# Top-p sets of an attention matrix: sorted lists of segment maxima in place of a 28-step bisection

## The chip, the cores and the metric

One core of a Trainium2 chip runs the whole program. The metric is the device time of one execution in microseconds (us), as a median of several executions. The engines are named PE (TensorE, matrix products), DVE (VectorE), ACT (ScalarE), POOL (GpSimd) and SP (SyncE, which issues most transfers). In the traces here, where all products are float32, each leaves two records (the 8 logits products of a tile are 16 records at 574.39 us of the kernel before), so a count behind PE is twice the number of products in the code.

## The reference, cut to what matters

Four layers work on 4096 nodes with 256 features and a 4096x4096 adjacency matrix, in float32. Layer 1 is the one that the change touches. It makes two attention steps, and each row keeps the smallest set of largest probabilities that reaches 0.9:

```python
def _top_p_attention(X, W1, W2, W3):
    q = X @ W1.T @ W2.T
    k = X @ W3.T
    probs = softmax(q @ k.T, axis=-1)                  # 4096 x 4096
    idx = argsort(-probs, axis=-1)
    sp = take_along_axis(probs, idx, axis=-1)
    cs = cumsum(sp, axis=-1)
    keep_sorted = cs - sp < 0.9                        # sum of all larger ones is below 0.9
    mask = zeros(...).at[rows, idx].set(keep_sorted)
    A = probs * mask
    return A / maximum(A.sum(-1, keepdims=True), 1e-12)

Xf, Xa = X, X
for n in range(2):
    A = _top_p_attention(Xa, W1, W2, W3)
    Xf = R @ Xf                                        # R: row-normalised adjacency + identity
    Xa = A @ Xa
    Z = Z + Xf @ U1[n].T + Xa @ U2[n].T
```

Layer 0 before it and layers 2 and 3 after it are the same in both kernels. Among equal probabilities those with the lower index are kept first. In step 2 this matters: a count on the host, which no run shows, finds some 860 rows with equal values at the border of the set, because rows whose attention keeps a single neighbour become copies of one another.

## The kernel before

A row is one of 128 partitions, and a tile is 128 rows, so each step has 32 tiles. `e` holds a tile's exponentials, 4096 a partition, and there are two such tiles. The threshold is found bit by bit: for each of 28 bits one pass over all 4096 elements sums what lies at or above a candidate. (Cuts are marked.)

```python
T_BASE, T_BITS = 0x30000000, 28

def bisect(e, tgt, cand, bits):
    for b in bits:
        junk = tmp_tile([P, N], BF16)
        f = small.tile([P, 1], F32, name="f")
        nc.vector.scalar_tensor_tensor(junk, e, cand.bitcast(F32), e, op0=OP.is_ge, op1=OP.mult, accum_out=f)
        up = small.tile([P, 1], I32, name="up")
        nc.vector.tensor_scalar(up, f, tgt, float(1 << b), op0=OP.is_ge, op1=OP.mult)
        nc.vector.scalar_tensor_tensor(cand, cand, (3 << b) >> 1, up, op0=OP.bitwise_xor, op1=OP.bitwise_xor)

# ... keep_top: one more pass, then per 1024 columns an equality, a scan, two masks and a sum

def weighted_sum(ps, e, rhs):
    for g in range(NT // 4):
        pt = psum.tile([P, 4, P], F32, name="pt", tag="tp", bufs=2)
        for k in range(4):
            j = g * 4 + k
            nc.tensor.transpose(pt[:, k, :], e[:, j * P:(j + 1) * P], ident)
        eT = work.tile([P, 4, P], F32, name="eT")
        nc.scalar.copy(eT, pt)
        for k in range(4):
            j = g * 4 + k
            nc.tensor.matmul(ps[:, :D], eT[:, k, :], rhs[j], start=(j == 0), stop=(j == NT - 1))

# in attn_step, for each tile I:
            bisect(e, tgt, cand, bits[:8])
            if pending is not None:
                step_out(*pending)                     # output products of the tile before
            adj_matmul(psr, Xf, I)                     # R @ Xf
            if I + 1 < NT:
                nxt = attn_prep(n, I + 1)              # logits and exponentials of the next tile
            bisect(e, tgt, cand, bits[8:])
            rk = keep_top(e, tgt, floor, cand)
            weighted_sum(psa, e, Xa)                   # A @ Xa
```

## Time and profile before

The time is 13,453 us. Cut at the first use of the bisection and at the end of each stage, the span divides like this:

| stretch | us | PE busy | DVE busy | granted PE clock |
|---|---|---|---|---|
| step 1 | 5760 | 29% | 96% | 0.63 |
| step 2 | 5765 | 27% | 96% | 0.62 |
| layer 2 | 830 | 77% | 88% | 0.88 |
| layer 3 | 539 | 99% | 12% | 1.00 |

Layer 0 takes the first 550 us or so. Read the table row by row: the busiest engine of a stretch is the candidate for its bound, and here DVE has no time left in either step. The lines that carry this are shown in the prediction below. One line belongs beside them, the clock granted to TensorE in 40 equal slices of the span, in tenths of full speed:

```profile
PEclk9998555555555555555666666666666666658899
```

TensorE was granted 0.63 and 0.62 of full speed through the two steps. It waits for VectorE there: in step 2 it stood idle for 3984 of 5765 us until VectorE's last masking of a tile was done.

### The profile page before, as it was taken

The page shows a single profiled execution, that of the slowest core. Times are in us where ns is not written, and L with a number is a line of the kernel's source. Part 1 is how long each engine was busy: PE and PEld are TensorE (multiplying, and loading weights), DVE is VectorE, ACT ScalarE, POOL GpSimd, SP SyncE. Part 2 cuts the span into 40 slices and gives each one's busy share as a digit, 9 for nine tenths or more (in the row PEclk, how much of TensorE's full clock was granted, in tenths as well). Part 3 has the DMA queues.
Part 4 walks back from the last instruction along what each step waited for, and adds up shares of the span by engine and source line. Part 5 has one row for each costly group of instructions (what it writes and reads, how often), then busy time and mean ns, then how long its engine had stood idle before and what let it go on. Part 6 is the DMA issues. An engine that isn't in the chain of part 4 may idle for free.

```text
span 13444.6 us, 59326 instructions
## 1 busy us (share of the span) xinstructions
PE 4912.1 (37%) x20320; PEld 3788.8 (28%) x20320; DVE 11941.8 (89%) x11136; ACT 1236.6 (9%) x1897; POOL 1009.2 (8%) x760
## 2 busy tenths in 40 slices
PE   9987221122222221112222222222222222217799
PEld 7766111111111111111222111222211122216678
DVE  1399999999999999999999999999999999998841
ACT  0000000000000000000000000000000000003310
POOL 0000000000000000000111001111100111114420
PEclk9998555555555555555666666666666666658899
DMA  4432000000000000000000000000000000004444
GB/s 141 126 97 77 1 1 1 1 1 1 1 1 1 1 1 1 1 1 4 14 14 14 7 13 14 14 14 14 14 7 13 14 14 14 13 27 157 163 133 132
DMA packets 607406, 430.09 MB, mean 32 GB/s; under 512 B 24832, under 2 KB 573712, under 8 KB 607104
## 3 DMA queue, kind: packets, MB, share of 16 engines
q1 hardware_dynamic: 601600, 419.53, 10.1%
q10 hardware_dynamic: 4608, 4.20, 0.1%
q8 instruction: 161, 2.64, 0.1%
q0 software_dynamic: 896, 2.57, 0.1%
q14 instruction: 141, 1.16, 0.0%
HBM read 415.71 MB, written 10.49 MB: 32 GB/s over the span
## 4 chain that ended last, share of the span: by engine, by line
DVE 77%; PE 14%; issue 4%; POOL 3%; DMA 1%; ACT 0%; SPq 0%; DVEq 0%; ACTq 0%; POOLq 0%
DVE tmp L208 52%; PE acc L105 6%; DVE tmp L229 4%; DVE up L210 3%; PE acc L121 3%; DVE tmp L232 2%; DVE e L233 2%; DVE e L234 2%; DVE tmp L219 2%; PE lg L192 2%; DVE cand L211 2%; DVE tmp L228 1%; POOL rs L142 1%; DVE tmp L342 1%; DVE nm L195 1%
## 5 line engine op out<-in xcount | busy, mean ns | idle before, releaser
L208 DVE SCALAR_TENSOR_TENSOR tmp<-e,cand 128x4096 bf16<-128x4096 f32 x1792 | 8052.4, 4494 | 57.4
L116 PE MATMUL pt<-ident,e 128*128 128x128 f32 x3072 | 534.8, 332 | 8213.8 <-DVE e L234 7817.6
L116 PEld LDWEIGHTS pt<-ident,e 128*128 128x128 f32 x3072 | 451.9, 172 | 8322.7 <-DVE e L234 7866.2
L118 ACT COPY eT<-pt 128x512 f32<-128x512 f32 x768 | 427.5, 588 | 10140.8 <-PE pt L116 10140.6
L121 PE MATMUL acc<-x,eT 128*128 128x256 f32 x4096 | 1112.4, 432 | 55.4 <-ACT eT L118 55.3
L105 PE MATMUL acc<-x,panel 128*128 128x256 f32 x4096 | 933.0, 387 | 57.4 <-DVE y L257 57.4
L121 PEld LDWEIGHTS acc<-x,eT 128*128 128x128 f32 x4096 | 872.0, 219 | 256.0 <-ACT eT L118 118.4
L105 PEld LDWEIGHTS acc<-x,panel 128*128 128x128 f32 x4096 | 787.6, 194 | 179.4 <-DVE y L257 68.7
L275 POOL MEMSET cand<- 128x1 int32 x64 | 6.2, 100 | 9161.5 <-DVE e L233 9161.5
L121 PE MATMUL acc<-xa,eT 128*128 128x256 f32 x2048 | 585.6, 449 | 19.1 <-ACT eT L118 19.1
L192 PE MATMUL lg<-kT,qi 64*128 64x512 f32 x1024 | 527.5, 626 | 3.2 <-ACT e L193 3.2
L121 PEld LDWEIGHTS acc<-xa,eT 128*128 128x128 f32 x2048 | 456.8, 229 | 127.7 <-ACT eT L118 50.3
L105 PE MATMUL acc<-xf,panel 128*128 128x256 f32 x2048 | 488.7, 403 | 4.4 <-DVE y L257 4.4
L105 PE MATMUL acc<-xw,panel 128*128 128x257 f32 x2048 | 477.3, 386 | 12.4 <-DVE xw L74 10.7
L229 DVE TENSOR_TENSOR_SCAN tmp<-ones,last,tmp 128x1024 f32<-128x1024 f32 x192 | 450.9, 2348 | 0.0
L105 PEld LDWEIGHTS acc<-xf,panel 128*128 128x128 f32 x2048 | 418.8, 206 | 68.9 <-DVE y L257 4.8
L210 DVE TENSOR_SCALAR up<-f,tgt 128x1 int32<-128x1 f32 x1792 | 380.7, 212 | 51.0
L105 PEld LDWEIGHTS acc<-xw,panel 128*128 128x128 f32 x2048 | 379.9, 191 | 76.6 <-issue 27.7
L173 DVE TENSOR_SCALAR r<-acc 128x1 f32<-128x1 f32 x32 | 5.1, 159 | 437.5 <-PE acc L105 437.5
L387 DVE TENSOR_TENSOR y<-y,pz 128x256 f32<-128x256 f32 x32 | 13.5, 421 | 420.1 <-PE pz L386 420.1
L341 POOL TENSOR_TENSOR e<-tmp,score_b 128x1024 f32<-128x1024 f32 x128 | 330.4, 2589 | 430.7 <-PE pt L116 211.8
L211 DVE SCALAR_TENSOR_TENSOR cand<-cand,up 128x1 int32<-128x1 int32 x1792 | 285.1, 159 | 54.6
(107 smaller groups left out, 5558.4 us busy)
## 6 DMA issues: line engine op xcount, KB each, us to landing
panel<-in_adjT SPq DMA_DIRECT2D x1024, 256.0 KB, 2.7
tmp<-in_adj SPq DMA_DIRECT2D x128, 512.0 KB, 3.6
tmp<-in_adjT SPq DMA_DIRECT2D x128, 512.0 KB, 4.8
z<-z SPq DMA_DIRECT2D x64, 128.0 KB, 1.9
x<-in_x ACTq DMA_DIRECT2D x32, 128.0 KB, 4.0
out<-o SPq DMA_DIRECT2D x32, 128.0 KB, 1.8
q<-q SPq DMA_DIRECT2D x64, 32.0 KB, 1.8
qi<-q SPq DMA_DIRECT2D x64, 32.0 KB, 2.0
```

The costliest lines, as they stand in the source:

```text
L105: nc.tensor.matmul(ps[:, :n], a[:, k, :], rhs[j], start=(j == 0), stop=(j == NT - 1))
L116: nc.tensor.transpose(pt[:, k, :], e[:, j * P:(j + 1) * P], ident)
L118: nc.scalar.copy(eT, pt)
L121: nc.tensor.matmul(ps[:, :D], eT[:, k, :], rhs[j], start=(j == 0), stop=(j == NT - 1))
L192: nc.tensor.matmul(ps, qi[r, :], kT[r, c * LC:(c + 1) * LC], start=True, stop=True)
L208: nc.vector.scalar_tensor_tensor(junk, e, cand.bitcast(F32), e, op0=OP.is_ge, op1=OP.mult, accum_out=f)
L210: nc.vector.tensor_scalar(up, f, tgt, float(1 << b), op0=OP.is_ge, op1=OP.mult)
L211: nc.vector.scalar_tensor_tensor(cand, cand, (3 << b) >> 1, up, op0=OP.bitwise_xor, op1=OP.bitwise_xor)
L219: nc.vector.scalar_tensor_tensor(junk, e, t, e, op0=OP.is_gt, op1=OP.mult, accum_out=g)
L229: nc.vector.tensor_tensor_scan(cs, ones.to_broadcast([P, CC]), eq, last, op0=OP.mult, op1=OP.add)
L232: nc.vector.scalar_tensor_tensor(eq, cs, tgt, eq, op0=OP.is_lt, op1=OP.mult)
L341: nc.gpsimd.tensor_mul(e[:, cols], a, sb[:, cols])
```

## The change

The intent is to replace 28 passes over 4096 elements by few passes and short lists. Each row is cut into 32 segments of 128. One instruction gives the 8 largest elements of a segment, so 32 of them give 256 candidates. From these, repeated "8 largest" and "replace these 8 by zero" instructions build a sorted list of the largest 40 (step 1) or 64 (step 2). A running sum along the list shows where 0.9 is passed. The largest dropped value `u` then masks the row. In step 2 the sets are wider, so a secant search with three passes first finds a bound `h` above which everything is kept, and the list covers what lies below. The result is only right if no segment hides a ninth element that belongs to the set, if the list was long enough, and if the bound's sum stays below 0.9. These are the proofs. They are counted per tile, and a branch repeats a tile by the old bisection where a row failed. The core of the diff, with cuts marked by "..." and comments added here:

```diff
-    small = ctx.enter_context(tc.tile_pool(name="small", bufs=3))
+    small = ctx.enter_context(tc.tile_pool(name="small", bufs=2))
...
+    def attn_exp(n, I):                    # no row maximum: exp straight from PSUM, with row sums
+        e = epool.tile([P, N], F32, name="e")
+        s8 = small.tile([P, N // LC], F32, name="s8")
+        logits(n, I, lambda c, ps: nc.scalar.activation(e[:, c * LC:(c + 1) * LC], ps, AF.Exp,
+                                                        accum_out=s8[:, c:c + 1]))
+        return e, s8
+    def bound(e, s, tgt):
...
+        for k in range(EVALS):             # EVALS = 3
...
+            nc.vector.scalar_tensor_tensor(junk, e, h, e, op0=OP.is_ge, op1=OP.mult, accum_out=f)
...                                         # about 14 operations of one element for the secant
+    def keep_few(n, I, e, s8):
...
+        if n == 0:
+            for g in range(NS):            # NS = 32 segments, SEG = 128
+                nc.vector.max(cand[:, g, :], e[:, g * SEG:(g + 1) * SEG])
+        else:
+            h = bound(e, s, tgt)
...
+            for c in range(2):
...
+                nc.vector.scalar_tensor_tensor(w, ec, h, ec, op0=OP.is_lt, op1=OP.mult, accum_out=low[:, c:c + 1])
+                for g in range(NS // 2):
+                    nc.vector.max(cand[:, c * (NS // 2) + g, :], w[:, g * SEG:(g + 1) * SEG])
...
+        for k in range(K // 8):            # K = TOP[n], TOP = (40, 64)
+            t8 = top[:, k * 8:(k + 1) * 8]
+            nc.vector.max(t8, left)
+            if k < K // 8 - 1:
+                nc.vector.match_replace(rest, t8, left, 0.0)
+                left = rest
...                                         # scan, sums, u and the count r of kept ties
+        if n == 0:
+            nc.vector.scalar_tensor_tensor(e, e, u, e, op0=OP.is_gt, op1=OP.mult)
+            return rk
...                                         # ties per segment, a threshold for each segment
+        for g in range(NS):
+            eg = e[:, g * SEG:(g + 1) * SEG]
+            nc.vector.scalar_tensor_tensor(eg, eg, ties[:, g:g + 1], eg, op0=OP.is_gt, op1=OP.mult)
+        nc.vector.tensor_scalar(drop, iota8, d, u, op0=OP.is_lt, op1=OP.mult)
+        nc.vector.match_replace(e[:, ::-1], drop, e[:, ::-1], 0.0)
...
         for I in range(NT):
...
+            adj_matmul(psr, Xf, I)
...
+            weighted_sum(psa, cur[0], Xa)
+            XA.append(new_xa(I, psa, cur[1]))
+            if I + 1 < NT:
+                cur = (nxt[0], keep_few(n, I + 1, *nxt))
+            if I + 2 < NT:
+                nxt = attn_exp(n, I + 2)
+        n_bad = failed(n)                  # failing rows of each tile, and their sum
+        with tc.If(nc.values_load(n_bad[0:1, NT:NT + 1]) > 0):
+            for I in range(NT):
+                with tc.If(nc.values_load(n_bad[0:1, I:I + 1]) > 0):
...                                         # bisection, weighted sum and output of this tile again
```

## The prediction

> **What bounds the kernel now.** I read the page from the top: busy shares, slices, the chain that ended last, the groups; then a table by stage, and timelines for unit costs. First the shares, the slices and the chain:
>
> ```profile
> PE 4912.1 (37%) x20320; PEld 3788.8 (28%) x20320; DVE 11941.8 (89%) x11136; ACT 1236.6 (9%) x1897; POOL 1009.2 (8%) x760
> ...
> PE   9987221122222221112222222222222222217799
> ...
> DVE  1399999999999999999999999999999999998841
> ...
> DVE 77%; PE 14%; issue 4%; POOL 3%; DMA 1%; ACT 0%; SPq 0%; DVEq 0%; ACTq 0%; POOLq 0%
> ```
>
> VectorE (DVE) is full from slice 3 to slice 36 while TensorE (PE) idles there; before and after, PE is full. So it is a stage that DVE bounds, between two that it doesn't. The groups name the work:
>
> ```profile
> L208 DVE SCALAR_TENSOR_TENSOR tmp<-e,cand 128x4096 bf16<-128x4096 f32 x1792 | 8052.4, 4494 | 57.4
> ...
> L210 DVE TENSOR_SCALAR up<-f,tgt 128x1 int32<-128x1 f32 x1792 | 380.7, 212 | 51.0
> ```
>
> 1792 is 28 halvings x 64 tiles (2 attention steps of 32). The table by stage (layer 0, step 1, step 2, layer 2, layer 3; I cut at the first bisection and at the last score of step 2) gives the lengths:
>
> ```profile
> 550.00:6310.00 5760.00, 1684.46 (x6517) 1234.53 (x6515) 5552.74 (x4874) 479.38 (x760) 36.44 (x69) 0.63 0.05 14
> 6310.00:12075.00 5765.00, 1538.23 (x5882) 1151.68 (x5882) 5532.02 (x5066) 427.85 (x628) 542.66 (x292) 0.62 0.04 13
> 12075.00:12905.00 830.00, 636.97 (x2997) 529.27 (x2998) 732.40 (x816) 257.98 (x313) 347.89 (x187) 0.88 0.45 157
> 12905.00:13444.00 539.00, 533.34 (x2510) 456.06 (x2508) 63.42 (x165) 34.49 (x71) 49.33 (x98) 1.00 0.45 131
> ```
>
> The two attention steps are 11,525 us, 180 us a tile; everything else, 1919 us, is not touched by the change. Unit costs for later, from timelines of TensorE at full clock, then of VectorE and GpSimd (POOL):
>
> ```profile
> 560.38 14.08 PE L105 MATMUL acc<-x,panel 128*128 128x256 f32 x64
> 574.39 7.37 PE L192 MATMUL lg<-kT,qi 64*128 64x512 f32 x16
> ...
> 12504.51 1.04 PE L116 MATMUL pt<-ident,e 128*128 128x128 f32 x8
> ```
> ```profile
> 5004.50 1.27 DVE L233 SCALAR_TENSOR_TENSOR e<-e,cand 128x1024 f32<-128x1024 f32 x1
> 5005.68 0.15 DVE L231 COPY last<-tmp 128x1 f32<-128x1 f32 x1
> 5005.74 1.28 DVE L232 SCALAR_TENSOR_TENSOR tmp<-tmp,tgt 128x1024 f32<-128x1024 f32 x1
> 5006.93 4.48 DVE L208 SCALAR_TENSOR_TENSOR tmp<-e,cand 128x4096 bf16<-128x4096 f32 x1
> 5011.34 0.09 DVE L208 DVE_READ_ACCUMULATOR tmp<-e,cand 128x1 f32 x1
> ```
> ```profile
> 9003.35 4.79 POOL L306 TENSOR_TENSOR y<-y,bb 128x256 f32<-128x256 f32 x1
> 9008.21 0.72 POOL L307 TENSOR_TENSOR y<-y,x 128x256 f32<-128x256 f32 x1
> ```
>
> What counts on VectorE is the distance from start to start: 1.18 us for 1024 elements[...], 4.41 for 4096, 0.06 for an independent one-element operation; a dependent one takes about 0.19.
>
> [...] the same addition took 4.79 us beside a bisection pass and 0.72 after it. [...]
>
> **The change, part by part.**
>
> Removed, per tile: 28 bisection evaluations of 4.97 us (4.41 + 0.08 + two small operations and their latency) = 139; the row maximum, 4.4; the equality scan and masking, about 32. That is nearly all of the 180 us. The exponential now takes no maximum and reads PSUM directly.
>
> Added in step 1, on VectorE per tile: 32 maxes of 128 elements, each 0.133 for the elements + 0.09 = 0.225, so 7.2; five maxes and four match-and-replaces over 256, which depend on each other: a max 0.44 (the start-to-start of a dependent 256-wide statistic is 0.46), a replacement 0.58 with its load, 4.5; some 12 small operations 2.2; one masking pass 4.4; two additions 0.8. Sum 19. That is far below what TensorE needs per tile: adjacency 64 passes x 0.22 = 14.1; weighted sum 64 x 0.22 = 14.1 and 32 transposes x 0.12 = 3.8; logits 16 x 0.44 = 7.0; output products 1.8, transposes 0.5, projections 1.2; waits for ScalarE's copies about 1. Sum 43.5. The instruction order of the built kernel backs it: TensorE always has the next adjacency product and logits between two weighted sums, and two e buffers let VectorE work a tile ahead. **Step 1 becomes bound by TensorE**: 32 x 43.5 + 11 for start and end = 1403 us.
>
> Added in step 2, on VectorE per tile: three evaluations x 4.53 = 13.6; 42 one-element operations of the secant, partly dependent, 5.2; two low passes of 2048, 4.7; 32 maxes 7.2; eight maxes and seven replacements over 256, 7.6; 25 small list and tie operations, 5.1; 32 maskings of 128 elements x 0.24 = 7.7; one replacement over 4096, 4.5; layer norms and additions of the output, 3.1, and waits for GpSimd there about 2 (1.41 of it is seen in the trace before). Sum 60.7. TensorE needs 43.5 - 1.2 = 42 beside it. The order of instructions shows pairs: VectorE starts the next tile's first two evaluations inside the list of every second tile. I followed one pair by hand: each exponential is ready 10 us or more before VectorE asks for it, so VectorE never waits for TensorE. **Step 2 stays bound by VectorE**: first tile ready after 67, 31 x 60.7 = 1882, tail 33: 1982 us.
>
> Other: two proofs with their branches[...]. No branch is in this trace; I allow 10 us, a guess. Layer 2 loses its early loads, 5. The store of x in layer 0 hides under its matmuls.
>
> Sum: layer 0 up to the first logits 552; step 1 1403; step 2 1982; 10 + 5; layers 2 and 3 1369; 8 between span and reported time. **5329, which I round to 5320.**
>
> **The rivals.**
>
> 1. *Rows fail the proof.* A tile with one failing row costs 139 + 4.4 + 3.9 + 7 + 29 + 18 + 8, and 14 in step 2: about 225 us, all serial. 32 such tiles in step 2 would bring 12,500, and in both steps the gain is gone. I evaluated the tests in float32 on the reference's inputs, in ordinary arithmetic: no row of 4096 fails in either step. The closest in step 2 are a sum that passes its target by 0.1% and a bound 6e-6 below it; random logit errors up to 1e-4 in 12 trials failed no row. I give 3% to any failure.
> 2. *The new list operations run at two cycles an element.* Then maxes and replacements in step 2 take about 12.5 us more a tile, 400 us: 5720. In step 1 the 27 us still hide. [...]
> 3. *TensorE's clock.* In step 2 it idles for over 10 us before a weighted sum, so part runs cold. If all did, 42 would become over 80 us a tile and bound the step: 6000. [...]
> 4. *Handing over in turn* (VectorE's list, then the weighted sum): 60 + 42 a tile, 6650. Two e buffers and the order speak against it.
>
> **Range and chances.** Step 1 is built from measured rates, +-40. Step 2 hangs on 32 + 8 maxes, 8 replacements and 67 small operations not in the trace: 60.7 may be 53 to 69, +-260. So 5060 to 5600. Faster by over 2% is certain but for mass failure of the proof: 0.99.
>
> **What would show it.** TensorE 9 in all slices of step 1, clock near 1.0, VectorE about 45% busy, 43 to 45 us a tile. In step 2 VectorE above 93% busy, TensorE at 70 to 80%, 58 to 64 us a tile; a max of 128 starting every 0.22 us, a replacement over 4096 in 4.5. No bisection instruction at all. Wrong if: a bisection group appears; VectorE shows idle time released by TensorE in step 2; or the two steps' lengths are far from 1400 and 1980 even though their sum fits.

## More of the kernel before

The order in which the text issues work is not the order on the engines. A scheduler places the instructions of each engine when the kernel is built.

## The result, and the profile after

The changed kernel took 5279.95 us (5274.57 to 5282.53, 4 runs), against 13,450.9 us in the runs of the kernel before beside it. The ratio is 0.3924, with a 95% interval of 0.3919 to 0.3930. Ratios here are the mean time of one kernel's fast runs over that of the other's of the same rounds, so they are not quite the ratios of the medians. The output is correct.

The busy shares and slices of the changed kernel, to be laid beside those of the kernel before:

```profile
PE 4580.9 (87%) x20324; PEld 3559.5 (67%) x20324; DVE 3201.4 (61%) x8919; ACT 1161.2 (22%) x2345; POOL 822.0 (16%) x761
...
PE   8999999999999997887788787878647777789999
...
DVE  1000444444444428999999999999968899971111
...
PEclk9999999999999997988888888888878888989999
```

TensorE does the same work in less busy time (4581 instead of 4912 us), because its clock is back, 0.93 on average over the span instead of 0.67: 20,324 records instead of 20,320, and the four more are the two products that count the failing rows. The digit of VectorE is 4 in step 1 (slices 5 to 14) and 9 in step 2 (slices 17 to 29). That is a change of bound in the middle of the kernel: TensorE first, VectorE after. The two steps in the table by stage have the columns start and end, length, then busy us and instructions of PE, PEld, DVE, ACT and POOL, and at the end granted clock, DMA share and GB/s:

```profile
552.00:1971.00 1419.00, 1416.62 (x6384) 1050.77 (x6383) 573.95 (x1967) 367.43 (x932) 36.67 (x67) 1.00 0.18 53
1971.00:3881.00 1910.00, 1461.61 (x5986) 1094.99 (x5984) 1750.28 (x5740) 459.89 (x896) 341.29 (x291) 0.87 0.13 38
```

TensorE is busy for 1416.6 of 1419 us in step 1. VectorE is busy for 92% of step 2. No bisection instruction is in the trace: no row failed a proof.

The pace of a step is read from an instruction that comes once a tile. Its summary gives count, shortest, median and longest duration in ns, and the starts of the first and the last. These two are the addition that ends a tile of step 1, and the replacement over the whole row that ends a list in step 2:

```profile
L494 DVE TENSOR_TENSOR z<-pz,x x32: 423/425/425, 625.9 to 1963.4; 128x256 f32<-128x256 f32 x32
...
L389 DVE MATCH_REPLACE8 e<-drop,e x32: 4404/4409/4414, 2065.4 to 3841.6; 128x4096 f32<-128x4096 f32 x32
```

Step 1 runs at (1963.4 - 625.9) / 31 = 43.15 us a tile, step 2 at (3841.6 - 2065.4) / 31 = 57.3. These two figures, and the head of step 2 (from the last addition of step 1 to the first replacement, 102 us), serve to compare all experiments below.

Now the unit costs that no line of the old trace could show, from VectorE's timeline of the changed kernel (start, duration, and a count where like instructions are run together):

```profile
3002.84 6.28 DVE L337 MAX8 cand<-tmp 128x8 f32<-128x128 f32 x32
...
3009.88 0.41 DVE L349 MATCH_REPLACE8 rest<-top,cand 128x256 f32<-128x256 f32 x1
3010.33 0.43 DVE L347 MAX8 top<-rest 128x8 f32<-128x256 f32 x1
...
3027.79 1.66 DVE L386 SCALAR_TENSOR_TENSOR e<-e,ties 128x128 f32<-128x128 f32 x6
```

The 32 maxes fill 6.28 us, 0.193 us from start to start. A group of maskings of the same width needs more: the 6 in the last line take 1.66 us, of which the last alone is 0.35, so one starts every 0.263 us. The loading of a replacement's eight values is an instruction of its own, 0.09 us before a replacement over 256 that takes 0.41. All of VectorE's time in step 2 can be split like this. I took the stretch of 31 tiles between the ends of the first and the last replacement, gave each instruction the time up to the next one's start, and counted what went beyond an instruction's own end as idle:

| VectorE, us a tile in step 2 | predicted | measured |
|---|---|---|
| three evaluations (90 of 93 fall into the stretch) | 13.6 | 12.9 |
| secant, one-element operations | 5.2 | 4.9 |
| two passes below the bound | 4.7 | 4.6 |
| 32 maxes of 128 | 7.2 | 6.2 |
| sorted list, 8 maxes and 7 replacements of 256 | 7.6 | 6.5 |
| small list and tie operations | 5.1 | 4.1 |
| 32 maskings of 128 | 7.7 | 8.4 |
| replacement over 4096 | 4.5 | 4.5 |
| output: additions, layer norms, score | 3.1 | 2.5 |
| idle, nearly all of it before the output's operations | 2.0 | 2.8 |
| sum | 60.7 | 57.4 |

The head of step 2 is worth a look of its own. TensorE and VectorE at the branch, with idle time before an instruction and its releaser in brackets:

```profile
1970.64 2.40 PE L115 MATMUL acc<-xf,panel 128*128 128x256 f32 x10 [1.68 <-PEq L473]
1977.57 27.64 PE L206 MATMUL lg<-kT,qi 64*128 64x512 f32 x32 [4.54 <-DMA qi<-q]
```
```profile
1992.31 0.16 DVE L322 TENSOR_REDUCE f_s<-s 128x1 f32<-128x8 f32 x1 [26.65 <-ACT e L268]
```

All five engines load the count and come to the branch of line 473 between 1965.7 and 1968.5 us, and none starts an instruction of its own between 1969.0 and 1970.6. The branch itself holds TensorE for only 1.7 us. But the load of `q` for the first tile was issued behind it, at 1975.5 us, and TensorE waited 4.5 us for that. Then 32 logits records take 0.86 us each, at a granted clock of 0.50, and VectorE sits idle for 26.7 us until the first exponentials are there.

### The profile page after: what moved, and what is told of

It reads as the page before. It is cut to its first block, busy times and chain, and to the rows that moved or that the text cites. A ratio compares the mean times of both kernels' runs of the same rounds, so it can differ in the third digit from the quotient of the medians.

```text
span 5276.1 us, 57582 instructions
## 1 busy us (share of the span) xinstructions
PE 4580.9 (87%) x20324; PEld 3559.5 (67%) x20324; DVE 3201.4 (61%) x8919; ACT 1161.2 (22%) x2345; POOL 822.0 (16%) x761
## 5 line engine op out<-in xcount | busy, mean ns | idle before, releaser
L131 PE MATMUL acc<-x,eT 128*128 128x256 f32 x4096 | 1018.1, 400 | 33.5 <-ACT eT L128 33.1
L131 PEld LDWEIGHTS acc<-x,eT 128*128 128x128 f32 x4096 | 781.4, 198 | 239.3 <-ACT eT L128 128.7
L126 PE MATMUL pt<-ident,e 128*128 128x128 f32 x3072 | 444.5, 290 | 383.5 <-DVE e L389 199.2
L328 DVE MAX8 cand<-e 128x8 f32<-128x128 f32 x1024 | 221.2, 280 | 670.6 <-ACT e L268 670.6
L115 PE MATMUL acc<-xw,panel 128*128 128x257 f32 x2048 | 478.2, 387 | 12.4 <-DVE xw L84 11.5
L281 DVE SCALAR_TENSOR_TENSOR tmp<-e,h 128x4096 bf16<-128x4096 f32 x96 | 432.9, 4510 | 0.0
L354 POOL COPY f_x<-ex 128x1 f32<-128x1 f32 x64 | 75.3, 1177 | 1816.5 <-DVE ex L353 1738.6
L150 POOL TENSOR_SCALAR ve<-mv 128x1 f32<-128x1 f32 x160 | 88.2, 551 | 1640.0 <-DVE mv L148 1167.3
L206 PEld LDWEIGHTS lg<-kT,qi 64*128 64x128 f32 x1024 | 163.1, 189 | 265.3 <-ACT e L268 179.7
L268 ACT ACTIVATE e<-lg 128x512 f32<-128x512 f32 x512 | 305.3, 599 | 150.7 <-PE lg L206 150.7
L386 DVE SCALAR_TENSOR_TENSOR e<-e,ties 128x128 f32<-128x128 f32 x1024 | 271.6, 346 | 0.0
```

What stands on the lines that cost most here:

```text
L115: nc.tensor.matmul(ps[:, :n], a[:, k, :], rhs[j], start=(j == 0), stop=(j == NT - 1))
L206: nc.tensor.matmul(ps, qi[r, :], kT[r, c * LC:(c + 1) * LC], start=True, stop=True)
L268: logits(n, I, lambda c, ps: nc.scalar.activation(e[:, c * LC:(c + 1) * LC], ps, AF.Exp, accum_out=s8[:, c:c + 1]))
L281: nc.vector.scalar_tensor_tensor(junk, e, h, e, op0=OP.is_ge, op1=OP.mult, accum_out=f)
L328: nc.vector.max(cand[:, g, :], e[:, g * SEG:(g + 1) * SEG])
L386: nc.vector.scalar_tensor_tensor(eg, eg, ties[:, g:g + 1], eg, op0=OP.is_gt, op1=OP.mult)
```

## The experiments

All results of these kernels were correct. Times are medians of 2 to 5 runs; a difference of less than 12.5 us, the widest spread among the runs of one kernel, is not told from noise by the time alone. Pace and head are read from the same two instructions as above.

| run | time | step 1, us a tile | head of step 2 | step 2, us a tile |
|---|---|---|---|---|
| changed kernel | 5279.95 | 43.15 | 102 | 57.3 |
| no_branch | 5239.6 | 43.3 | 68 | 57.4 |
| max2 | 5417.6 | 43.1 | 108 | 61.4 |
| max3 | 5595.4 | 43.2 | 114 | 67.0 |
| logits2 | 5525.0 | 49.7 | 118 | 57.4 |
| in_turn | 5340.5 | 44.8 | 93 | 58.4 |
| one_e | 6269.9 | 44.8 | 78 | 88.7 |
| fail7 | 6837.5 | 43.1 | 99 | 56.3 |
| out_dve | 5256.5 | 43.1 | 103 | 56.5 |
| wide_masks | 5177.4 | 43.2 | 99 | 54.2 |
| wide_out | 5139.6 | 43.2 | 99 | 52.9 |
| warm_first | 5270.2 | 43.2 | 90 | 57.4 |

### Which engine bounds which step: max2, max3 and logits2

Work was doubled on one engine at a time, by issuing the same instruction twice.

```diff
 # max2, in both steps (max3: three times)
                 nc.vector.max(cand[:, g, :], e[:, g * SEG:(g + 1) * SEG])
+                nc.vector.max(cand[:, g, :], e[:, g * SEG:(g + 1) * SEG])
 # logits2
             nc.tensor.matmul(ps, qi[r, :], kT[r, c * LC:(c + 1) * LC], start=True, stop=True)
+            nc.tensor.matmul(ps, qi[r, :], kT[r, c * LC:(c + 1) * LC], start=True, stop=True)
```

> Each of the 32 maxes over 128 elements is issued twice in both steps, so VectorE gets 32 x 0.193 = 6.2 us more a tile, and the result stays right. Theory (step 1 bound by TensorE, step 2 by VectorE): step 1 gains at most its first tile's 6 us, step 2 gains 32 x 6.2 = 198 us; in all 5485 us. Rival (step 2 is by now held as much by hand-overs and TensorE as by VectorE): step 2 gains under 100 us. Second rival (step 1 hands over late as well): step 1 gains over 50 us.

> Each logits product is issued twice in both steps (the second overwrites the first with the same values), so TensorE gets 7.0 us more a tile, and the result stays right. It is the mirror of the doubled maxes. Theory: step 1 gains 32 x 7.0 = 224 us, step 2 only its start, up to 25 us at the cold clock, its pace staying at 57 to 58 us a tile; in all 5520 us. Rival (step 2 is near balance, since TensorE is 77% busy there at a granted clock of 0.87): step 2 gains over 100 us, in all over 5600 us.

logits2 fell as the theory said, 5525 us for 5520 expected. Its two pace lines, the addition of step 1 and the replacement of step 2:

```profile
L495 DVE TENSOR_TENSOR z<-pz,x x32: 423/424/426, 644.5 to 2185.5; 128x256 f32<-128x256 f32 x32
...
L390 DVE MATCH_REPLACE8 e<-drop,e x32: 4401/4408/4414, 2303.6 to 4082.2; 128x4096 f32<-128x4096 f32 x32
```

Step 1 went from 43.15 to 49.7 us a tile, 6.6 for the 7.0 us of products added, and step 2 stayed at 57.4 with the same addition. In step 1 all of TensorE's work is on the path, in step 2 it is hidden. For max2 the mirror image held in step 1: 6.2 us a tile more on VectorE changed nothing (43.13). But in step 2 the pace rose by 4.1 us, not 6.2, and the total missed its expectation by 67 us. Splitting VectorE's time as before shows that the maxes did grow, from 6.2 to 12.4 us a tile, while idle time fell from 2.8 to 1.8, the secant from 4.9 to 4.4 and the small list operations from 4.1 to 3.7. Of the idle time, 0.8 us had been waits for TensorE's output products, and these are gone; of the secant's one-element operations 43 took over 0.4 us in the changed kernel and one does in max2. So about 2 us a tile of waits and blocked operations were displaced by the added work. A third copy of the maxes tests whether that was a stock used up once:

> Each of the 32 maxes is issued three times. Doubling them had cost 4.1 us a tile in step 2 where they are 6.2. Theory (the first doubling was partly swallowed by VectorE's waits for GpSimd, 2.8 to 1.8 us idle a tile, and by fewer blocked operations, and these are now used up): another 6.2 us a tile, 67.6 us, 5615 us. Rival (each doubling costs only two thirds of its length, so VectorE is not what bounds step 2): 65.5 us a tile, 5550 us.

The replacements of max2 and then of max3, first and last start:

```profile
L391 DVE MATCH_REPLACE8 e<-drop,e x32: 4401/4406/4416, 2070.9 to 3974.0; 128x4096 f32<-128x4096 f32 x32
```
```profile
L393 DVE MATCH_REPLACE8 e<-drop,e x32: 4401/4406/4411, 2077.1 to 4154.1; 128x4096 f32<-128x4096 f32 x32
```

The second addition cost 67.0 - 61.4 = 5.6 us a tile of the 6.2 added, in all 5595 us where the theory said 5615 and the rival 5550. VectorE bounds step 2, and its waits give back about 2 us a tile when other work is put beside them. The missing 0.6 us is not explained.

### What lets the two engines work side by side: in_turn and one_e

in_turn writes the loop without any looking ahead:

```diff
-        cur = attn_exp(n, 0)
-        cur = (cur[0], keep_few(n, 0, *cur))
-        nxt = attn_exp(n, 1)
...
-            weighted_sum(psa, cur[0], Xa)
-            XA.append(new_xa(I, psa, cur[1]))
-            if I + 1 < NT:
-                cur = (nxt[0], keep_few(n, I + 1, *nxt))
-            if I + 2 < NT:
-                nxt = attn_exp(n, I + 2)
+            e, s8 = attn_exp(n, I)
+            rk = keep_few(n, I, e, s8)
+            weighted_sum(psa, e, Xa)
+            XA.append(new_xa(I, psa, rk))
```

> The exponential and the list of a tile are put just before the same tile's weighted sum, so no tile is worked ahead; the arithmetic is the same and the result stays right. Theory (the two steps owe their length to two e tiles in work at once): in step 1 VectorE's 17 us of list come on top of TensorE's 43, 60 us a tile; in step 2 some 52 us of VectorE on top of TensorE's 42, 94 to 100 us a tile; in all about 1400 + 550 in step 1 and 1900 + 1200 in step 2, 7030 us. Rival (the order matters little, since adjacency products and output work still lie beside the list): under 6300 us.

My theory fell: 5340 us, 60 us more and not 1750. TensorE's timeline of this run in step 1 tells why:

```profile
1017.82 4.92 PE L206 MATMUL lg<-kT,qi 64*128 64x512 f32 x10
1022.68 11.92 PE L115 MATMUL acc<-x,panel 128*128 128x256 f32 x54
1035.18 1.09 PE L126 MATMUL pt<-ident,e 128*128 128x128 f32 x8 [0.58 <-DVE e L368]
1036.11 0.60 PE L115 MATMUL acc<-x,panel 128*128 128x256 f32 x2
```

Between the logits of a tile and its transposes lies an adjacency product, and its last pieces go between the groups of the weighted sum. The scheduler puts the next tile's work there, although the text has it later, as far as a free buffer lets it. So the order of the text was not what the overlap hangs on, though it is not without effect: step 1 is 1.6 us a tile slower, which makes 50 of the 60 us. one_e takes the buffer away:

```diff
 # in_turn, and in addition
-    epool = ctx.enter_context(tc.tile_pool(name="epool", bufs=2))
+    epool = ctx.enter_context(tc.tile_pool(name="epool", bufs=1))
 # attention steps use one tag, layer 2 alternates between two
-        e = epool.tile([P, N], F32, name="e")
+        e = epool.tile([P, N], F32, name="e", tag="e0")
```

> As the run in turn, but the attention steps have a single e tile (layer 2 keeps its two), so that the next tile's exponentials cannot be written before TensorE has transposed the last of the present one, whatever order the scheduler picks. The result stays right. Theory (it is the second e tile that lets VectorE and TensorE work side by side): in step 2 some 52 us of list, then 17 of transposes and products, then 8 of logits follow one another, 77 us a tile, +640 us; step 1 hides most of its list beside the adjacency product, +0 to +160 us; in all 6000 to 6150 us. Rival (not the buffer either; the adjacency product alone would cover it): under 5500 us.

It took 6270 us, 929 more than in_turn and nearly all of it in step 2: 88.7 us a tile. TensorE's and VectorE's timelines of one tile there:

```profile
3009.62 7.72 PE L115 MATMUL acc<-xf,panel 128*128 128x256 f32 x35
3059.39 1.97 PE L126 MATMUL pt<-ident,e 128*128 128x128 f32 x8 [42.05 <-DVE e L389]
3061.18 5.73 PE L131 MATMUL acc<-xa,eT 128*128 128x256 f32 x16
```
```profile
3086.87 0.42 DVE L499 TENSOR_TENSOR y<-pz,z 128x256 f32<-128x256 f32 x1 [27.54 <-PE pz L448]
```

TensorE waits 42 us for the end of VectorE's list, and VectorE waits 27.5 us in its turn. The second `e` tile is what the overlap of step 2 hangs on, as the theory had it. The size was off: I had 25 us between the last replacement and the next evaluation, and it was 34 (from 3059.3 to 3093.2). Two things add to my sum: after 42 us of idling the first 8 transposes take 1.97 us, where the next group takes 1.04, and the first 16 products 5.73 instead of 3.72; and the output products of the tile before go between the logits. Step 1 did not suffer from the single buffer at all, 44.8 us a tile in both runs.

### What the branches cost: no_branch

```diff
-        with tc.If(nc.values_load(n_bad[0:1, NT:NT + 1]) > 0):
...
```

> Both branches and their bodies are taken out; the proofs are still computed. No row fails on these inputs, so the result stays right. Theory (read from the trace of the changed kernel): the branch lets no engine run ahead, so step 2 starts with an idle VectorE and a cold TensorE. Its first tile took 99 us where I had predicted 67, and layer 2's first weighted sum came 76 us after the last score where it was 56 before. Expect -30 us at the head of step 2 and -20 us at the head of layer 2, in all 5230 us, and the pace of 57.3 us a tile in step 2 unchanged. Rival (my blind guess of 10 + 5 us): 5265 us, the late start being the fault of step 2's own data dependences and not of the branch.

It took 5239.6 us, 40 us less. The head of step 2 shrank from 102 to 68 us, where -30 was expected. The time from the last replacement of step 2 to layer 2's first result shrank from 112.7 to 100.7 us: the first layer 2 result came 55 us after the last score instead of 76, but the last score came 9 us later. TensorE at the same place without the branch:

```profile
1970.26 8.72 PE L206 MATMUL lg<-kT,qi 64*128 64x512 f32 x18
1978.91 13.65 PE L115 MATMUL acc<-xf,panel 128*128 128x256 f32 x62
```

Logits records take 0.48 us each here, at a granted clock of 1.00, part of them was done before the last tile of step 1 ended, and nothing is idle. The rival, my 15 us of the prediction, falls: the two branches cost about 40 us although no body is ever run. The run does not separate the stop from the data that a body would change: it writes `q` and the step's results anew, so the loads after it have to wait for it in any case.

### Whether it is the clock: warm_first

```diff
+        if n:
+            warm = psum.tile([P, D], F32, name="warm", tag="ms", bufs=2)
+            for j in range(24):
+                nc.tensor.matmul(warm, ident, X[j], start=(j == 0), stop=(j == 23))
         cur = attn_exp(n, 0)
```

> At the head of step 2, ahead of the first logits, TensorE gets 24 products of the identity with 128x256 tiles whose result nobody reads; the result stays right. In the changed kernel the 32 logits records at the head of step 2 took 27.6 us, 0.86 us each, in one unbroken stretch at a granted clock of 0.50, where the same products took 0.48 each in the run without branches. Theory (the idle 1.7 and 4.5 us at the barrier let the clock fall, and logits products, which fill only 64 of 128 rows, do not bring it back): after the full-array products the logits run at 0.45 to 0.50 us each, 32 in about 15 us; the total hardly moves, since the 24 products take 11 to 20 us themselves: 5265 to 5295 us. Rival (these logits are slow for another reason, for instance their reads beside the DMA traffic at the barrier): they stay at 0.86 us, and the total rises by 10 us or more.

The head of step 2 on TensorE:

```profile
1970.47 10.60 PE L455 MATMUL warm<-x,ident 128*128 128x256 f32 x48 [1.72 <-PEq L477]
1981.00 15.28 PE L206 MATMUL lg<-kT,qi 64*128 64x512 f32 x32
```

The 32 logits records took 15.3 us instead of 27.6, and the granted clock was 1.00 instead of 0.50. The products ran in the time that TensorE had waited for `q`, and the head of step 2 shrank from 102 to 90 us although 10 us of useless work were added. The time, 5270.2 us, is 10 us less, which alone would be within the noise. That the clock was the reason for the slow logits is shown. In the changed kernel the 10 adjacency records behind the branch still had 1.00, the 4.4 us of idling after them 0.89 on average, and all 27.6 us of unbroken logits 0.50. In the adjacency records that followed the clock was 0.50 up to 2010 us, 0.93 on average from 2010 to 2015, and 1.00 from there to 2028. Why it stayed at 0.50 under the logits is not shown: they fill 64 of the 128 rows and the adjacency products fill all, and no run changes that alone.

### What a failing row costs: fail7

```diff
-TOP = (40, 64)
+TOP = (40, 56)
```

> The list of step 2 is cut from 64 to 56 entries. On the host's arithmetic 7 rows, each in another tile, then fail the proof in step 2, and none in step 1; the branch repairs them and the result stays right. Theory (my prediction's price of a failing tile): 7 x 223 = 1561 us more, less 32 x 1.0 us for one max and one replacement fewer: 6810 us. Rival (the bisection body is as dear as a tile of the kernel before, 180 us): 7 x 180 = 1260 us more, 6510 us.

It took 6837.5 us, 1557.6 more. The bisection group of this run's page, and the table's row for the stretch from the usual last score (start, end, length, then busy times as above):

```profile
L226 DVE SCALAR_TENSOR_TENSOR tmp<-e,cand 128x4096 bf16<-128x4096 f32 x196 | 878.8, 4484 | 6.8
```
```profile
3845.00:5423.00 1578.00, 324.81 (x1310) 242.11 (x1309) 1227.82 (x1111) 97.55 (x140) 33.38 (x62) 0.60 0.04 10
```

196 evaluations are 28 for each of 7 tiles, so seven tiles failed, as many as the host's arithmetic gave; that they are the same seven, with one row in each, the trace does not show. They take 1578 / 7 = 225 us each, the figure of the prediction. A tile in the branch is dearer than a tile of the kernel before (180 us), and little lies beside it: TensorE is busy for 325 of 1578 us. One failing row costs a whole tile.

### Shortening VectorE's work in step 2: out_dve, wide_masks and wide_out

```diff
 # out_dve
-        nc.gpsimd.tensor_mul(h, h, gb)
-        nc.gpsimd.tensor_add(h, h, bb)
-        nc.gpsimd.tensor_add(h, h, X[I])
+        nc.vector.tensor_mul(h, h, gb)
+        nc.vector.tensor_add(h, h, bb)
+        nc.vector.tensor_add(h, h, X[I])
 # wide_masks: NM = 8 segments of MSEG = 512; ties summed over 32 candidates instead of 8
-        for g in range(NS):
-            eg = e[:, g * SEG:(g + 1) * SEG]
+        for g in range(NM):
+            eg = e[:, g * MSEG:(g + 1) * MSEG]
 # and one more proof, since 8 ties at most can be dropped
+            nc.vector.scalar_tensor_tensor(ok, facts["d"], 8.5, ok, op0=OP.is_lt, op1=OP.mult)
```

> The three operations of 128x256 on GpSimd in step 2's output (times gain, plus bias, plus X) go to VectorE; the result stays right. VectorE gets 3 x 0.33 = 1.0 us a tile more work. Theory (GpSimd's operations and VectorE's two-input ones keep each other waiting, as 2.8 us of idle VectorE a tile before the output's operations show, and as single-element operations of 0.58 to 0.72 us beside GpSimd show): about 2 us a tile of waits go, net -1 to -2 us a tile, 5220 to 5250 us. Rival (the idle time is a dependence that stays when the work moves): +1.0 us a tile, 5310 us.

> Step 2 masks 8 segments of 512 instead of 32 of 128; ties are counted over the wider segments, with one more test in the proof that at most 8 are dropped in the segment where they end; the result stays right. Theory (the fixed part of each masking is 0.13 us on VectorE, and VectorE sets the pace): 32 x 0.263 = 8.4 becomes 8 x (0.533 + 0.13) = 5.3, -3.1 us a tile, some 5180 us. Rival (the masks end just before TensorE may start, so that something else sets the pace): less than half of it, over 5230 us.

> Both the wider masks and the output's operations on VectorE; the result stays right. If both theories hold, the gains add, since both shorten VectorE's work on the path: -4 to -5 us a tile, 5120 to 5150 us. If TensorE's 42 us a tile at a granted clock of 0.87 begins to show, less than the sum of the two single runs.

Moving three operations to VectorE, its own bound, made step 2 faster: 5256.5 us, -0.8 us a tile. The added operations cost 1.0 us there, idle time fell from 2.8 to 1.8 and the secant from 4.9 to 4.4. Of the idle time about half went with GpSimd's additions, and half with waits for TensorE's output products (0.8 to 0.3). What the secant loses is seen in the changed kernel, where some operations of one element take four times their usual 0.15 us and more while one of GpSimd's runs: 43 of the secant's 1320 take over 0.4 us, and in out_dve none does. All 43 are SCALAR_TENSOR_TENSOR instructions that read two tensors, and each overlaps one of GpSimd's three operations. First GpSimd's timeline, then VectorE's:

```profile
3041.09 0.72 POOL L506 TENSOR_TENSOR y<-y,gb 128x256 f32<-128x256 f32 x1 [0.53 <-DVE na L287]
```
```profile
3041.12 0.72 DVE L288 SCALAR_TENSOR_TENSOR b<-h,na 128x1 f32<-128x1 f32 x1
```

The gain is smaller than the theory's, -23 us where 30 to 60 were expected, but the rival's +30 is excluded.

The wider masks gave -3.1 us a tile, 5177.4 us, as expected. The masking line of that run:

```profile
3039.53 5.39 DVE L388 SCALAR_TENSOR_TENSOR e<-e,ties 128x512 f32<-128x512 f32 x8
```

Eight maskings fill 5.4 us where 32 filled 8.4. The elements are the same 4096, so the 24 instructions that are gone were worth 0.13 us each. (The 0.533 us in the expectation is 512 x 1.04 ns, an estimate from the changed kernel's replacements: 4.41 us for 4096 elements and 0.41 for 256.) Both together reach 5139.6 us, 0.3819 of the kernel before (interval 0.3814 to 0.3824), where the changed kernel has 0.3924. That is 2.7% below the changed kernel, and the best version here. The gains add and a little more (-4.4 us a tile for -3.1 and -0.8), so at 52.9 us a tile TensorE's 42 does not show yet.

## Why the prediction was right

5320 us were predicted and 5280 measured, 0.8% apart, so the range of 5060 to 5600 held and so did "faster". The agreement is closer than the terms deserve, and that is luck: the pace of step 2 was put 106 us too long, while the other terms together were put some 60 us too short. By its own steps:

- **Layer 0, 552 us.** The first logits came at 551.4. Right.
- **Step 1 becomes bound by TensorE, 1403 us.** 1419 were measured. The mechanism is shown by logits2 and max2. The pace was 43.15 where 43.5 was predicted. The two ends took 81 us, that is 1419 - 31 x 43.15, where one tile and 11 us, 54.5, had been given to them. TensorE waited for only 2.4 us in the whole step, so this is no wait: it does the logits of three tiles and the adjacency products of two before the first addition. VectorE was 40% busy, a little below the expected 45%.
- **Step 2 stays bound by VectorE, 1982 us.** 1910 were measured, and the mechanism is right (logits2, max3, wide_masks). The size of the pace was off: 57.3 us a tile for 60.7, just outside the 58 to 64 that the prediction named as its sign. The table of VectorE's time shows where: maxes of 128 took 0.193 us and not 0.225, the sorted list and the small operations about 1 us less each, and only the maskings more, 0.263 instead of 0.24. In 31 tiles this is -106 us. The idle time was 2.8 us for 2, and not all of it is for GpSimd. Small waits for TensorE's output products, 0.8 us a tile, are among them, so "VectorE never waits for TensorE" was too strong, though no exponential came late after the head. Such waits were one of the prediction's own signs of being wrong; by that sign this part of it was wrong, by 0.8 of 57.3 us a tile, which leaves the bound as it is. VectorE's share, 92%, is just under its 93%.
- **First tile ready after 67 us.** It took 99 (from 1971 to the end of the first replacement at 2070). Here the branch failed as a step: without branches the head is 34 us shorter, which makes 65.
- **Branches 10 us, layer 2's lost early loads 5.** In proportion this is the term that was mis-sized most. no_branch measures 40 us for both. I had thought of the stop itself, which is indeed only 1.7 us on TensorE. What I left out is that everything which usually runs ahead starts from nothing after it: the load of `q`, the logits at a granted clock of 0.50, and the exponentials before VectorE can begin. The clock's part of that is shown by warm_first.
- **Layers 2 and 3, 1369 us.** 1395 were measured, and the later start of layer 2 explains most of the difference.
- **The rivals.** No row failed; fail7 confirms the price of 225 us a tile and, for its seven tiles, the host's count. The list operations do not take twice the time for an element: a replacement takes 4.41 us for 4096 elements and 0.41 for 256, 1.04 ns for each one more, as the old kernel's bisection and masking passes do (4.41 us for 4096, 1.18 for 1024, so 1.05 ns). A max of 128 took 0.193 us, and twice 1.04 ns would alone make 0.27. A cold TensorE did not bound step 2, which ran at a granted clock of 0.87; part of it was cold, as the 6 us from 2069 on, which had 0.50 after 16.9 us of idling. Handing over in turn did not happen, and of the two reasons I gave, two buffers and the order, the buffers count for 929 us and the order for 60 (one_e, in_turn).
- **Two readings and an assumption.** The prediction says that the same addition took 4.79 and 0.72 us on GpSimd. Its lines show two additions of one size, L306 and L307, and not one; the comparison holds, with 4.53 and 0.73 us on average over 32 tiles. Its starts of VectorE's passes, 4.41 us for 4096 elements and 1.18 for 1024, give 1.05 ns an element and leave 0.10 us that does not grow with them, an estimate from those two. The 0.133 us for the elements of a max is an estimate too, 128 x 1.04 ns, from the durations of 4.48 us for 4096 elements and 1.28 for 1024. That a max goes at that rate, the 0.09 us beside it and the 0.58 of a replacement with its load were my assumptions; no line of the old trace shows them.

The sum: 5329 predicted before rounding, then +16 in step 1, -106 for the pace of step 2, +34 for its head and tail, -10 for the branch term that is now in the head, +21 in layers 2 and 3, and -4 between span and time, gives 5280.

## What to carry to other kernels

When a bound is taken away, work out for each stage which engine is next, from the sums of both: here the same change left one stage to TensorE and the other to VectorE, and only in the latter was further trimming of VectorE worth anything. The branches, whose bodies never ran, still had a price, 40 us for two here; count the chain of load, first products at a low clock (0.50 here) and first results behind them, not the jump. What let two engines overlap here was the second buffer far more than the order of the text, and an expectation drawn from the order of the source should be checked against the order on the engines.
